# The front of layer 0: where U's loads, U's products and adj's first loads stand in a planned kernel

## The chip, the cores and the metric

The kernel runs on one core of one Trainium2 chip. The metric is the device time of one execution in microseconds (us), the median of several runs. The program has five engines that run side by side, each in the order of its own instruction queue: TensorE (PE, with its weight loads shown as PEld), VectorE (DVE), ScalarE (ACT), GpSimd (POOL), and SyncE (SP), which issues nearly all of the DMA transfers.

## What is computed

Two graph layers on 3327 nodes with 256 features, all in float32. In the program the nodes are padded to 26 row tiles of 128. Layer 0 is the layer that the change touches, and within it step n = 0 and what comes before it:

```python
h = maximum(layernorm(x), 0)                    # X, the input of layer 0
R = (adj + I) / rowsum(adj + I)
Xf = Xa = X;  Z = 0
for n in range(2):
    q = Xa @ W1.T @ W2.T;  k = Xa @ W3.T
    A = top_p(softmax(q @ k.T), 0.9)            # rows renormalised
    Xf = R @ Xf
    Xa = A @ Xa
    Z = Z + Xf @ U1[n].T + Xa @ U2[n].T
x = x + layernorm(X + Z)
...                                             # layer 1: masked attention over neighbours
```

## The kernel before, in words

**Order of the work.** The kernel is a list of pieces. Each piece is put into a plan with `put(engine, length, rank, fn, needs, take, give, lag)`: an assumed length, a rank (lower goes first), the pieces that it needs, the buffers that it takes and gives back, and a lag after its end until others may use its result. `Plan.order` (L507 on) then steps through assumed time: whenever an engine is free, it takes, of the pieces that are ready and whose buffers are free, the one with the lowest rank. The result is one fixed order per engine; on the chip each engine runs that order strictly, and waits on semaphores for what it really needs. `either` puts a piece that the plan gives to ACT or to DVE, whichever comes free for it first. So an assumed length, rank or lag changes no work, but changes the order in the queues.

**The front.** SP loads the 26 row tiles of x into `rhs` (`load_x`, L1962, rank -200 + t), with the two halves of U among them (in `weights`, L713 to L720; the trace shows the issue under L584): U1[0] and U1[1] side by side in `u1`, 128 x 2 x 512. ACT's queue loads W1, W2 and W3; PE and ACT make `wqk` of them (L724 to L745). For each row tile t there is then a chain: DVE measures mean and variance (L1213, L1214), POOL turns them into scale and bias in groups of 1 to 4 tiles (L1218 to L1221), ACT normalises and applies relu (L1239), PE transposes the tile into a `pl` bank (L1244), DVE copies it to `c[:, t]` (L1247), PE projects it to keys and queries in a `px` bank (L1252), ACT copies them to one of three `kq` buffers (L1258), POOL spreads the keys into `kt` (L1261), and SP stores or doubles the queries (L1269). A `kq` buffer comes back when POOL and SP are through with it. These pieces have rank -100 + t. Every fourth tile also goes through a small transpose and product in the two accumulator banks `acca` and `accf` (L789, L798, L808, L810).

**U's products.** Since R @ (X @ U) is (R @ X) @ U, the kernel multiplies the transposed tile `c[:, t]` by both halves of U first (`project_u`, L1304: four matmuls of 512 columns per tile, planned at 1.73 us). The left 256 columns of the result go to `main[:, t]`, the source of R's first product, and the right 256 over `c[:, t]`. The pieces of PE have rank -1.9 + 0.001 t: they fill PE's free time behind the chain of every tile and behind the logits of the first row (rank -2.5). The result stands in a `px` bank for t up to 7 and in `acca` or `accf` after that; ACT copies the left half (L1307), DVE the right half (L1308), both with rank -2.3.

**What follows.** `search` puts the logits of one row tile (L909) on PE, their exponentials and counts on ACT, DVE and POOL; `attention` multiplies the sparsified row by X (L1133) with `acca`; `full` multiplies a row tile of adj by `main` (L1158, 26 x 4 column groups of adj loaded by L1152 into six `at` buffers) with `accf`. `full` for n = 0 may load adj after all of the right-half copies of `project_u` (the argument `after`). SP loads U2 into the place of `u1` once the last of U's products is through (L747 to L752). 

**Idle work.** `idle` (L1966 to L1969) is a transpose of the identity into `accf` that nobody reads; 34 of these are put with rank 90, the last place in any choice, one after the other. They hold `accf` from the first to the last.

Of the kernel before, what the change touches and what calls it, by code (L numbers as in the profile page):

```python
# [19 lines left out]
P = 128  # L20
N = 3327
NT = 26
NP = NT * P
D = 256
# [563 lines left out]
def fast(  # L588
# [17 lines left out]
    nc = tc.nc  # L606
# [40 lines left out]
    with ExitStack() as l0:  # L647
# [53 lines left out]
        def weights():  # L701
            held = {}
            w1 = etpool.tile([P, 3 * D], F32, name="et")[:, : 4 * P].rearrange("p (a b) -> p a b", a=4)
            w1 = w1[:, 0, :].rearrange("p (c o) -> p c o", c=2)
            w2 = small.tile([P, PIECES, 8], F32, name="cands").rearrange("p c r -> p (c r)")[:DA, :DA]
            w1r = small.tile([P, PIECES * 8], F32, name="rest", bufs=1)[:DA].rearrange("p (k o) -> p k o", k=1)
            w1r = [w1r[:, 0, :], small.tile([P, P], F32, name="kq", bufs=BUFS["kq"])[:DA]]
            nc.scalar.dma_start(w1, w1t.rearrange("(c p) o -> p c o", p=P))
            nc.scalar.dma_start(w2, w2t)
            for r in range(2):  # L710
                nc.scalar.dma_start(wqk[:, :, r, r * DA : r * DA + DA], w3t.rearrange("(c p) o -> p c o", p=P))
            for n in range(STEPS):
                cols = slice((1 - n) * D, (2 - n) * D)  # L713
                uloads.append(
                    plan.put(
                        "SP", 0.4, -196.5 + n, nc.sync.dma_start, u1[:, :, cols],
                        u1t[n].rearrange("(c p) o -> p c o", p=P), lag=8.0,
                    )
                )

            S.activation(adds[:, 2:], powers[:, :1], AF.Exp)

            def turn():
                held["ps"] = ps_x.tile([DA, 2, P], F32, name="px")  # L724
                for k in range(2):
                    T.transpose(held["ps"][:, k, :], w1[:, k, :], ident)

            def copy():
                for k in range(2):
                    S.copy(w1r[k], held["ps"][:, k, :])  # L730

            def product():
                held["ps"] = ps_x.tile([P, 2, DA], F32, name="px")
                for k in range(2):
                    T.matmul(held["ps"][:, k, :], w1r[k], w2, start=True, stop=True)

            def place():
                for r in range(2):
                    S.copy(wqk[:, :, r, (1 - r) * DA : (2 - r) * DA], held["ps"])

            a = plan.put("PE", 0.25, -200.0, turn, take=["px"], needs=[plan.put("", 0.0, -201.0, lambda: None, lag=8.0)])
            a = plan.put("ACT", 0.5, -200.0, copy, needs=[a], take=["kq"], give=["px"])
            a = plan.put("PE", 0.25, -200.0, product, needs=[a], take=["px"], give=["kq"])
            return plan.put("ACT", 0.5, -200.0, place, needs=[a], give=["px"])
# [550 lines left out]
        def project_u(t, rank):  # L1295
            held = {}


            bank = ("acca", "accf")[t % 2] if t > 7 else "px"

            def product():
                ps = held["ps"] = (ps_x if bank == "px" else ps_a).tile([P, 2 * D], F32, name=bank)
                for k in range(2):
                    T.matmul(ps, c[:, t, k * P : (k + 1) * P], u1[:, k, :], start=(k == 0), stop=(k == 1))  # L1304

            a = plan.put("PE", 1.73, rank, product, needs=[turned_h[t], uloads], take=[bank])
            b = plan.put("ACT", 0.37, -2.3, lambda: S.copy(main[:, t, :D], held["ps"][:, :D]), needs=[a])  # L1307
            e = plan.put("DVE", 0.43, -2.3, lambda: V.tensor_copy(c[:, t, :], held["ps"][:, D:]), needs=[a])  # L1308
            plan.put("", 0.0, -2.6, lambda: None, needs=[b, e], give=[bank], lag=0.0)
            return b, e  # L1310

        def finish1(row, done, rank):
# [657 lines left out]

        spare = []
        a = plan.put("", 0.0, -202.0, lambda: None, lag=1.9)
        for k in range(34):
            a = plan.put("PE", 0.21, 90.0, idle, needs=[a], take=["accf"] * (k == 0), give=["accf"] * (k == 33), lag=0.0)

        uloads = []
        weighed = weights()
        loads = [plan.put("SP", 0.58, -200.0 + t, load_x, t) for t in range(NT)]
        measured = {}
        for lo, hi in zip(GROUPED, GROUPED[1:]):  # L1980
            measured.update(deviations(lo, hi))
# [8 lines left out]
        for n in range(STEPS):  # L1990
            base = 30.0 * n
            scaled = plan.put(
                "DVE", 0.2, base - 50.0,
                lambda gk=gks[n]: V.tensor_scalar(gk[:, : DA + 1], gk[:, : DA + 1], 1.0 / (-(-NT // 4) * P), None, ALU.mult), needs=[sums],
            )
            rows = [Row(n, i) for i in range(NT)]
            found = []
            held_by = []
            for g in range(GROUPS):
                lo, hi = 4 * g, min(4 * g + 4, NT)  # L2000
                r = base + lo - 6.0
                if n == 0 and g < 2:
                    q = saved[lo:hi]
                else:
                    q = plan.put(
                        "SP", 1.2, r, fetch_queries, n, g, needs=[saved[lo:hi], all_saved if n == 0 else None], take=["qg"], lag=3.0
                    )
                known, read = stats(n, lo, hi, base - 50.0 if g == 0 else r, [keys, q, fresh], scaled)
                found += [search(rows[t], base + t, [keys, q], known, fresh) for t in range(lo, hi)]
                plan.put("", 0.0, -90.0, lambda: None, needs=[read, [r.pieces["logits"] for r in rows[lo:hi]]], give=["qg"],  # L2010
                    lag=0.0,
                )
            if n == 0:
                drawn[0] = rows[-1].pieces["logits"]
            fulls = [
                full(n, t, (2.0 + 1.3 * t if n == 0 else base + 2.0 + 1.05 * t), [p[0] for p in sources], [p[1] for p in sources] if n == 0 else loaded[0])
                for t in range(NT)
            ]
            done = [attention(r, base + r.i, *found[r.i], right) for r in rows]
            failed.append(plan.put("DVE", 2.95, base + NT if n == 0 else 63.0, failures, n, needs=[[a for a, _ in found]]))  # L2020
            if n == 0:
                ends = [finish1(r, done[r.i], base + r.i + 0.2) for r in rows]
                stored = [y for _, _, _, y in ends]

                keys, after = [k for k, _, _, _ in ends], [drawn[0]]
                saved = [q for _, q, _, _ in ends]
                for r in range(2):
                    p = plan.put(
                        "SP", 1.3, base + NT, fetch_keys, r, needs=[after, saved[: LAST + 1]], lag=5.0
                    )  # L2030
                    keys.append(p)
                    after = [plan.put("", 0.0, -90.0, lambda: None, needs=[p], lag=0.0)]
                sums = [g for _, _, g, _ in ends]

                right, after = [], [done, stored]
                for lo in range(0, NT, 4):
                    hi = min(lo + 4, NT)
                    right.append(plan.put("SP", 0.1, base + NT, fetch_rhs, lo, hi, needs=after, lag=7.0))
                    after = [plan.put("", 0.0, -90.0, lambda: None, needs=right[-1:], lag=0.0)]
                fresh = failed + [r.pieces["guess"] for r in rows]  # L2040
                used, sources = sources, [(p,) for p in fulls]

                def layer1():
                    late["g"], late["b"], late["wa"], late["a"] = layer1_loads()

                    late["less"] = lambda: GP.tensor_scalar(late["b"], late["b"], -1.0, None, ALU.add)

                a = plan.put("SP", 1.8, base + NT + 1.0, layer1, needs=[used, stored], take=["et"], lag=8.0)
                less = plan.put("POOL", 0.6, base + 5.0, lambda: late["less"](), needs=[a])
                layer1_ready = plan.put(  # L2050
                    "DVE", 3.7, base + 5.0, lambda: layer1_scores(late["wa"], late["a"]), needs=[a], give=["et"],
                )
                layer1_ready = [layer1_ready, less]
            else:
                ends = [finish2(r, done[r.i], fulls[r.i], base + r.i + 0.2) for r in rows]
# [71 lines left out]
```

## Time and profile before

| what | value |
|---|---|
| median of 3 runs | 2057.34 us (2057.19 to 2058.23) |
| the profiled execution | 2056.36 us |
| its span, first to last instruction | 2054.5 us |
| PE busy | 2019.0 us, 98% of the span |
| DVE / ACT / POOL busy | 82% / 63% / 50% |
| granted TensorE clock, mean of the span | 0.998 |

The profile is one execution. A row gives the engine, the line of the kernel, the operation, output <- input, and how many; where it ends in square brackets, the engine stood idle so long before it, and the releaser that ended it follows. In the rows of a stretch, the busy time of each engine is followed by its instruction count, and then by PEclk, the granted TensorE clock (1.00 is full speed), the share of the DMA engines and what they moved. A PE instruction that is one of a run overlaps with the next, so the durations of single matmuls must not be added; the busy time of a stretch is a union and may be.

### The profile page before, as it was taken

To read this page: it belongs to the slowest core of one execution; us is meant where nothing else is said; L and a number is where in the kernel's file an instruction comes from. 1 tells how busy PE (TensorE), PEld (TensorE's weight loads), DVE (VectorE), ACT (ScalarE), POOL (GpSimd) and SP (SyncE) were. 2 spreads that over 40 slices of the span, in tenths; PEclk is the share of its full clock that TensorE was granted. 3 is DMA by queue.
4 is the path that set the end of the run, shared out by engine and by line. 5 is a ranking of instruction groups with operands and counts; after the bars stand their busy time and mean duration, and the time that the engine had idled before them with its cause. 6 is when DMAs were issued, how large, how long until landed. Compare 5 with 4: busy or idle time off the path is not lost. (4 is left out here: it accounts for less than half of the span.)

```text
span 2054.5 us, 34072 instructions
## 1 busy us (share of the span) xinstructions
PE 2019.0 (98%) x10545; PEld 1397.3 (68%) x10545; DVE 1691.5 (82%) x3753; ACT 1301.6 (63%) x2647; POOL 1029.3 (50%) x2222
## 2 busy tenths in 40 slices
PE   8999999999999999999999999999999999999997
PEld 6477877878777887788787787788877333333332
DVE  5488898888888854888887888978897999999894
ACT  4686667667576507884777787877643456474642
POOL 4366746565666504887766778877782000000001
PEclk9999999999999999999999999999999999999999
DMA  3177767767766776787676767766794354444440
GB/s 97 47 203 195 200 199 207 192 191 191 209 187 195 216 198 208 208 226 192 182 199 196 191 185 216 206 187 184 214 265 132 111 158 126 150 125 117 129 117 25
DMA packets 628991, 358.20 MB, mean 174 GB/s; under 512 B 366810, under 2 KB 581760, under 8 KB 628800
## 3 DMA queue, kind: packets, MB, share of 16 engines
q1 hardware_dynamic: 627904, 355.72, 61.6%
q8 instruction: 86, 1.41, 0.3%
q14 instruction: 105, 0.86, 0.1%
q10 hardware_dynamic: 896, 0.21, 0.0%
HBM read 252.69 MB, written 102.88 MB: 173 GB/s over the span
## 5 line engine op out<-in xcount | busy, mean ns | idle before, releaser
L964 ACT ACTIVATE junk<-e,sc 128x3327 fp8e5<-128x3327 f32 x147 | 451.0, 3068 | 62.7 <-POOL sc L1001 61.2
L1133 PE MATMUL acca<-rhs,e 128*128 128x256 f32 x2132 | 471.9, 380 | 3.6 <-DMA e<-blocks 3.5
L1133 PEld LDWEIGHTS acca<-rhs,e 128*128 128x128 f32 x2132 | 416.5, 196 | 50.2 <-issue 6.9
L1158 PE MATMUL accf<-main,at 128*128 128x257 f32 x1352 | 316.4, 383 | 7.4 <-ACT f L1169 2.6
L1158 PE MATMUL accf<-c,at 128*128 128x256 f32 x1352 | 308.4, 382 | 4.5 <-DVE main L1175 3.7
L1158 PEld LDWEIGHTS accf<-main,at 128*128 128x128 f32 x1352 | 249.9, 190 | 66.4 <-issue 18.9
L1158 PEld LDWEIGHTS accf<-c,at 128*128 128x128 f32 x1352 | 252.6, 190 | 54.0 <-issue 9.4
L1027 DVE MAX8 cands<-y 128x8 f32<-128x205 f32 (+1 forms) x832 | 242.8, 361 | 3.6
L1022 DVE SCALAR_TENSOR_TENSOR y<-e,sc 128x1639 f32<-128x1639 f32 x84 | 168.6, 2008 | 71.8 <-POOL sc L1012 70.8
L1738 ACT ACTIVATE junk<-at 128x448 bf16<-128x448 f32 (+1 forms) x204 | 112.2, 550 | 178.1 <-DVE e L1749 109.3
L1928 POOL TENSOR_TENSOR qq<-qq 128x256 f32<-128x256 f32 x4 | 2.9, 729 | 429.9 <-ACT qq L1924 429.9
L1765 PE MATMUL pl<-e,main 128*64 128x416 f32 x1024 | 192.2, 517 | 0.0
L909 PE MATMUL pl<-kt,qg 64*128 64x512 f32 (+1 forms) x832 | 174.2, 536 | 1.2 <-ACT e L926 1.0
L1078 DVE SCALAR_TENSOR_TENSOR e<-e,thr 128x1024 f32<-128x1024 f32 (+1 forms) x126 | 172.8, 1373 | 1.3 <-DVE rest L1072 0.4
L1117 DVE STREAM_TRANSPOSE e<-e 128x1024 f32<-128x1024 f32 (+1 forms) x123 | 164.5, 1338 | 7.2 <-POOL sc L1004 0.5
L926 ACT ACTIVATE e<-pl 128x1024 f32<-128x1024 f32 x123 | 134.7, 1105 | 53.2 <-PE pl L909 50.0
L1765 PEld LDWEIGHTS pl<-e,main 128*64 128x64 f32 x1024 | 69.0, 137 | 109.5 <-issue 91.7
L1749 DVE SCALAR_TENSOR_TENSOR e<-qq,low,junk 128x832 f32<-128x832 f32 x128 | 129.5, 1076 | 4.4 <-ACT junk L1738 2.8
L1749 DVE SCALAR_TENSOR_TENSOR e<-c,low,junk 128x832 f32<-128x832 f32 x128 | 129.1, 1071 | 4.2 <-issue 3.2
L909 PEld LDWEIGHTS pl<-kt,qg 64*128 64x128 f32 x832 | 71.3, 186 | 87.5 <-issue 72.4
L1133 PE MATMUL acca<-rhs,qq 128*128 128x256 f32 x520 | 115.0, 380 | 0.3 <-DVE thr L1069 0.3
L1737 ACT ACTIVATE at<-at 128x448 f32<-128x448 f32 (+1 forms) x204 | 110.3, 540 | 0.0
(554 smaller groups left out, 3375.4 us busy)
## 6 DMA issues: line engine op xcount, KB each, us to landing
at<-in_adjt_dram SPq DMA_DIRECT2D x414, 256.0 KB
blocks<-e SPq DMA_DIRECT2D x82, 512.0 KB
e<-blocks SPq DMA_DIRECT2D x328, 128.0 KB
blocks<-e SPq DMA_DIRECT2D x41, 640.0 KB
e<-blocks SPq DMA_DIRECT2D x164, 160.0 KB
at<-in_adjt_dram SPq DMA_DIRECT2D x102, 192.0 KB
blocks<-qq SPq DMA_DIRECT2D x20, 512.0 KB
qq<-blocks SPq DMA_DIRECT2D x80, 128.0 KB
```

The source lines that it names most:

```text
L909: T.matmul(pl[:, lo : lo + m], qg[self.n, self.i // 4][half, self.i % 4, :], kt[half, 512 * k : 512 * k + m], start=True, stop=True,)
L926: S.activation(to, pl.rearrange("p (g t q) -> p g t q", g=4, t=2), AF.Exp, accum_out=sums[k])
L964: S.activation(junk[:, :N], self.e[:, :N], fn, bias=t, scale=-1.0, accum_out=dst, saturate=False)
L1022: V.scalar_tensor_tensor(self.y[:, : hi - lo], self.e[:, lo:hi], self.up, self.e[:, lo:hi], ALU.is_lt, ALU.mult, accum_out=(self.h0, self. ...
L1027: V.max(self.cands[:, a * PIECES // 2 + k, :], self.y[:, at[k] - lo : at[k + 1] - lo])
L1078: V.scalar_tensor_tensor(piece, piece, self.thr[:, at : at + 1], piece, ALU.is_gt, ALU.mult)
L1117: V.transpose(part, part)
L1133: T.matmul(self.acc, lhs, rhs[self.n][:, j, :], start=(j == 0), stop=(j == NT - 1))
L1158: T.matmul(self.acc[:, : self.w], self.at[j // JC][:, j % JC, :], self.src[:, j, : self.w], start=(j == 0), stop=(j == NT - 1),)
L1738: S.activation(to, src, AF.Sign)
L1749: V.scalar_tensor_tensor(held["e"][:, k, :], extra["both"][b % 2][:, k, :], low[:, j, k : k + 1], held["mask"], ALU.max, ALU.mult,)
L1765: T.matmul(q["acc"][a][k * FH : (k + 1) * FH, c, :C], main[:, j, h * FH : (h + 1) * FH], held["e"][:, h, c * C : (c + 1) * C], start=(j == 0),
```

## The change

It reorders the front, in five places. U's two loads go behind the second tile of x, ahead of the third, and the plan is told shorter lags for them, for x and for W1. U's results all go to `acca` and `accf` in turn, none to `px`. Their two copies get ranks t - 97, next to the chains of tiles t to t + 3, and each may go to ACT or to DVE; the empty piece that gives the bank back goes to rank -300. The idle transposes are 15 in place of 34. And adj's loads for n = 0 need the stored queries (`saved`) in place of U's right-half copies.

```diff
@@ weights
                     plan.put(
-                        "SP", 0.4, -196.5 + n, nc.sync.dma_start, u1[:, :, cols],
-                        u1t[n].rearrange("(c p) o -> p c o", p=P), lag=8.0,
+                        "SP", 0.4, -198.5 + 0.1 * n, nc.sync.dma_start, u1[:, :, cols],
+                        u1t[n].rearrange("(c p) o -> p c o", p=P), lag=4.5,
                     )
...
-            a = plan.put("PE", 0.25, -200.0, turn, take=["px"], needs=[plan.put("", 0.0, -201.0, lambda: None, lag=8.0)])
+            a = plan.put("PE", 0.25, -200.0, turn, take=["px"], needs=[plan.put("", 0.0, -201.0, lambda: None, lag=5.0)])
@@ project_u
-            bank = ("acca", "accf")[t % 2] if t > 7 else "px"
+            bank = ("acca", "accf")[t % 2]
...
             a = plan.put("PE", 1.73, rank, product, needs=[turned_h[t], uloads], take=[bank])
-            b = plan.put("ACT", 0.37, -2.3, lambda: S.copy(main[:, t, :D], held["ps"][:, :D]), needs=[a])
-            e = plan.put("DVE", 0.43, -2.3, lambda: V.tensor_copy(c[:, t, :], held["ps"][:, D:]), needs=[a])
-            plan.put("", 0.0, -2.6, lambda: None, needs=[b, e], give=[bank], lag=0.0)
+            b, e = (
+                plan.either(
+                    ("ACT", 0.37, lambda to=to, k=k: S.copy(to[:, t, :D], held["ps"][:, k * D : (k + 1) * D])),
+                    ("DVE", 0.43, lambda to=to, k=k: V.tensor_copy(to[:, t, :D], held["ps"][:, k * D : (k + 1) * D])),
+                    t - 97.0, needs=[a],
+                )
+                for k, to in enumerate((main, c))
+            )
+            plan.put("", 0.0, -300.0, lambda: None, needs=[b, e], give=[bank], lag=0.0)
             return b, e
@@ fast
-        for k in range(34):
-            a = plan.put("PE", 0.21, 90.0, idle, needs=[a], take=["accf"] * (k == 0), give=["accf"] * (k == 33), lag=0.0)
+        for k in range(15):
+            a = plan.put("PE", 0.21, 90.0, idle, needs=[a], take=["accf"] * (k == 0), give=["accf"] * (k == 14), lag=0.0)
...
-        loads = [plan.put("SP", 0.58, -200.0 + t, load_x, t) for t in range(NT)]
+        loads = [plan.put("SP", 0.48, -200.0 + t, load_x, t, lag=2.2 if t < 2 else 3.5) for t in range(NT)]
...
-                full(n, t, (2.0 + 1.3 * t if n == 0 else base + 2.0 + 1.05 * t), [p[0] for p in sources], [p[1] for p in sources] if n == 0 else loaded[0])
+                full(n, t, (2.0 + 1.3 * t if n == 0 else base + 2.0 + 1.05 * t), [p[0] for p in sources], saved if n == 0 else loaded[0])
```

## The prediction

> **What bounds the kernel now.** I read the page's busy shares and slices first: PE 98%, near full clock everywhere. So the stage rows come next; then the front by stretches, the waits of PE in it, and its PE queue in order of time.
>
> Stretches of the whole span, PE's busy time being the second figure:
>
> ```profile
> 0.00:5.91 5.91, 3.69 (x19) 3.45 (x19) 1.99 (x7) 2.09 (x3) 3.58 (x26) 1.00 0.62 164
> 5.91:97.77 91.86, 83.99 (x359) 47.57 (x359) 45.41 (x167) 53.38 (x140) 36.76 (x105) 0.98 0.22 63
> ```
> ```profile
> 100.00:750.00 650.00, 645.32 (x2962) 510.01 (x2961) 552.55 (x1384) 424.73 (x800) 389.47 (x844) 1.00 0.72 201
> 750.00:820.00 70.00, 69.87 (x327) 55.23 (x328) 22.15 (x86) 37.66 (x74) 23.59 (x55) 1.00 0.60 182
> 820.00:1520.00 700.00, 690.76 (x3200) 564.55 (x3198) 588.43 (x1501) 512.38 (x970) 536.42 (x1143) 1.00 0.73 200
> ```
>
> The reader is to see that PE stands 4.7 us in 650, 0.1 in 70 and 9.2 in 700, but 7.9 us (91.86 less 83.99) in the 92 us of the front. The end is PE's work plus PE's standing time. The row of 750 to 820 says that this also holds where the two steps meet: DVE has only 22 us of work there and PE is full, since products of `full` left over from step 0 still run. A search that begins some us sooner or later is covered by these; a PE microsecond saved in the front is saved at the end.
>
> Not all busy time of the front is work. PE's queue there, and the stretch around it (granted clock third from the right):
>
> ```profile
> 6.19 0.82 PE L1969 MATMUL accf<-ident 128*128 128x128 f32 x6
> ...
> 18.34 3.58 PE L1304 MATMUL acca<-late,c 128*128 128x512 f32 x4
> ...
> 23.08 1.88 PE L1304 MATMUL accf<-late,c 128*128 128x512 f32 x4
> ```
> ```profile
> 4.65:8.06 3.41, 2.52 (x20) 2.04 (x19) 1.73 (x7) 1.20 (x2) 2.71 (x9) 1.00 0.99 293
> ...
> 14.89:18.30 3.41, 1.98 (x15) 1.34 (x13) 2.89 (x13) 1.58 (x3) 2.95 (x9) 1.00 0.65 203
> 18.30:21.72 3.42, 3.42 (x6) 1.38 (x5) 2.79 (x11) 1.90 (x5) 2.15 (x8) 0.50 0.07 17
> ```
>
> The same four matmuls take 3.58 us at half clock and 1.88 at full; the half clock follows a stretch in which PE was busy 1.98 of 3.41 us, 58%. And the waits of PE from 5.9 to 98:
>
> ```profile
> PE accf L1158 <- DVE cands L1027: 2.4, 1, 2.4
> PE pl L1244 <- ACT rhs L1239: 2.2, 4, 0.9
> PE pl L1244 <- DVE bst L1213: 1.1, 1, 1.1
> PE pl L909 <- ACT e L926: 1.0, 1, 1.0
> ```
>
> The first is put down to a DVE instruction that has nothing to do with `accf`; what came last is adj's first tile: SP issues it at 92.08 and `full` starts at 97.77.
>
> **What can be saved.** From PE's first useful matmul (5.91) to the first one of `full` (97.77): standing 7.9; 15 idle transposes at some 0.14 us each (six in 0.82), 2.1; half clock, half of 3.4 us, 1.7. Together 11.7 us. What lies ahead of 5.91 (x's first tile, its statistics on DVE, POOL, ACT) the change leaves alone.
>
> **The change part by part.**
>
> *U's loads and W1's lag.* Before, the first product of U runs at 18.34, though `c` holds a tile from 8.35 on (the copy of 7.96): up to t = 7 the products need a `px` bank, which the chains of rank -100 take first. After: the two loads are issued at about 1.7 and 2.1 (x's issues are 0.45 us apart from 0.72); x2, issued about there now, is used 3.4 us later (4.99), so I put their landing near 5.5. The shorter assumed loads and lags of x move nothing by themselves but the order, and are costed with it. Tile 0 is normalised at 5.26 to 5.86, transposed by 6.35; its copy stands behind tile 2's statistics on DVE. I put the first product at 7.4. The loads are moved past x2 and x3 on SP (one also past x4): two issues of 0.38 us and 512 KB at the 290 GB/s of these stretches, 1.8 us for x2 and x3, 0.9 for x4, nothing from x5 on. The statistics of x2 so come at about 6.5 instead of 4.99, those of x4 at 7.33 as before. The cover is the first products, 1.7 us each; without them PE would stand those 1.8 us. W1's turn (7.84) and `wqk` (12.0) come some 3 us sooner; their transfers have long landed, since no row shows PE waiting for them.
>
> *Products as filler from 7.4 on.* Work per tile on PE: 0.39 (L1244: 10.2 over 26), 0.56 (L1252: 14.6 over 26) and 1.73, so 2.7 us. DVE needs 1.0 us per tile (0.41, 0.18, 0.41), ACT 0.86, the loads 0.45. Tiles come more than twice as fast as PE can use them, so standing in 8 to 22 should nearly vanish, and with it the half clock at 18.3 and the idle transposes. The 26 products are the same work as before, only sooner.
>
> *Banks.* The products lose `px`, which 8 of 26 used, most of them at 68 to 82. With two banks, one comes back after left and right copy one behind the other (0.37 and 0.42 us, DVE's mostly waiting for ACT's), about 1.0 us after the product; a cycle of 2.8 us on two banks, one product per 1.4, is less than the 1.73 that PE needs. So the cost is nothing while the copies are prompt. Where ACT is in a count of 3.07 us (L964), or DVE in one of 1.95 (L1022), a copy may come up to 3 us late, and PE stands for what exceeds 0.7. Bounds: 0 (81.9 to 91 runs on `acca` and `accf` alone, and stands nowhere) and 3 counts at 2.3, some 7. The nearest row is the first; I take 0.6.
>
> *Copies with rank t - 97.* The same 52 copies. New is who is queued behind them: a copy whose product isn't ended holds up the relu, the `kq` copy and the statistics of later tiles on its engine. Before, ACT waited 12.7 us for products in 0 to 60 (13 copies; 1.0 each). The price lies between nothing (PE has turned tiles in stock) and the rival below; I take 0.7 of PE time.
>
> *Idle transposes, 34 to 15.* They end at 1.78 + 15 x 0.19 = 4.6 instead of 5.47, and none fills 6 to 10. The Trainium skill (TensorE: Matmul & The Clock Gate, "Part 4: PE-mode transpose") says that transposes do not count as PE activity for the clock; by that, taking 19 away costs nothing. The trace disagrees: from 1.78 to 11.9 PE runs hardly anything but transposes and is granted 1.00 all through. So they count, and from 4.6 to 8.0 PE would have only some 1.3 us of tile 0, tile 1 and W1 and 0.6 of the first product, under 60%, like 14.89 to 18.30, which was followed by half clock. The same page's table in "Why this matters for your kernels" asks only for no gaps over about 3 us; by that no drop, by the row one drop of 3.4 us, 1.7 lost. I take the row: 1.7, bounds 0 and two stretches, 3.4.
>
> *adj's first loads.* Six issues move from 92 to behind the last query store, about 55, ahead of U2's two on SP. DMA share there is 0.00 to 0.16, so 1.5 MB are hidden. U2's loads still wait for the last product; behind them stand only loads whose `at` buffers are free no sooner. The 2.4 us go; the 1.0 before the logits too, since `full` can run there. Next late is the single bank of `full`, 0.5 us at a change of row tile: one more of these, 0.5.
>
> **Sum.** Left over: idle before the first product 0.2 to 0.8, taken 0.5; banks 0.6; copies 0.7; clock 1.7; bank of `full` 0.5: 4.0. Gain 11.7 - 4.0 = 7.7 us. The profiled execution (2054.5 of span and 1.86 around it) goes from 2056.4 to 2048.7; the median is 1.0 above the profiled one, so 2049.6. Everything behind is planned anew from other times; its 14 us of standing (4.7 + 0.1 + 9.2) may move by 4 either way.
>
> **Rivals.** *It does less than it says:* tiles reach `c` late, for DVE is in order and its statistics wait for x (5.3 us of that in the trace), so the holes of 8 to 18 stay; only adj's part (3.4) and half the transposes (1.0) count: 2057.3 - 4.4, 2053. For: DVE is 2.9 of 3.4 us busy in 8 to 18; against: its copies already come at 8, 9.8, 10.7, 12.1. *Nothing is left to lose in the front:* no clock drop and the steps pack better by 3 us: 2045. *Slower: the copies block the chain.* If each pair makes ACT stand 1 us in the stretch of the chains, 26 us come on top of ACT's 22 us of relu and `kq` copies in 5 to 40, 48 in 35: PE starves 13 us, against 7.7 gained, 2063. It decides from the point where waiting on ACT exceeds the 13 us that it has free, half of the pairs. For: strict queues, and the wait is there now; against: `either` spreads it over two engines, and product work covers it.
>
> **Numbers.** Forecast 2049.6, 50%; less than it says, 2053, 22%; everything, 2045, 14%; slower or given back later, 2058 to 2063, 14%. Range 2044.5 to 2057.5. A difference under 0.2% (4.1 us) can't be told from none: faster 0.74, same 0.14, slower 0.12.
>
> **What would show it.** Right: L1304 first at 7 to 8; PE busy over 95% from 8 to 22; no wait of `accf` L1158 near the end of the front; that first matmul at 89 to 91; a half clock, if any, before 12. Wrong: PE waiting in front of L1244 for ACT with copies of L1307's kind queued there; PE waiting for bank copies behind L964; or a front shorter by 8 us and standing in 100 to 1520 grown by as much.

## The result, and the profile after

| | before | after |
|---|---|---|
| median on one chip, 9 runs each | 2057.34 us (2055.35 to 2060.71) | 2050.47 us (2049.43 to 2054.74) |
| the profiled execution | 2056.36 us | 2050.93 us |
| its span | 2054.5 us | 2049.1 us |
| PE busy | 2019.0 us | 2017.5 us |
| granted TensorE clock, mean of the span | 0.998 | 0.996 |

The ratio is 0.9966, with a 95% interval of 0.9958 to 0.9975: the changed kernel is faster by 6.9 us in the medians and by 5.4 in the two profiled executions. The forecast was 2049.6. In the kernel after, lines behind L1304 stand some lines further down: the idle transposes are L1975, U's copies L1309 (ACT) and L1310 (DVE), layer 1's products L1771 (L1765 before).

PE's queue in the front of the kernel after, in order of time:

```profile
1.78 3.25 PE L1975 MATMUL accf<-ident 128*128 128x128 f32 x15 [1.78 <-POOL ident masks.py:199]
4.87 0.38 PE L726 MATMUL px<-ident,et 128*64 128x128 f32 x2
...
7.80 3.53 PE L1304 MATMUL acca<-late,c 128*128 128x512 f32 x4 [0.90 <-DVE c L1247]
...
14.13 1.95 PE L1304 MATMUL accf<-late,c 128*128 128x512 f32 x4
```

The first product of U runs at 7.80 (18.34 before), and it is the one that falls into the half clock: its four matmuls take 3.53 us, where those of the next take 1.95. The waits of PE from 0 to 100 us, with the total, the number and the longest:

```profile
PE accf L1975 <- POOL ident masks.py:199: 1.8, 1, 1.8
PE acca L1304 <- DVE c L1247: 0.9, 1, 0.9
PE pl L1244 <- ACT rhs L1239: 0.6, 1, 0.6
PE accf L1158 <- ACT f L1169: 0.5, 1, 0.5
PE acca L789 <- ACT kq L1258: 0.4, 1, 0.4
```

The 2.4 us of `accf` at the front's end are gone; the 0.5 is a change of `full`'s row tile at 99.17, behind the front. The same stretches as before the change (the front ends at the first product of `full`, now at 83.55):

```profile
5.88:83.55 77.67, 76.26 (x326) 44.35 (x326) 37.86 (x149) 47.22 (x123) 31.33 (x92) 0.98 0.25 73
...
100.00:750.00 650.00, 647.79 (x2980) 514.42 (x2979) 548.29 (x1373) 420.14 (x796) 403.04 (x841) 1.00 0.73 202
750.00:820.00 70.00, 68.42 (x320) 51.42 (x319) 32.45 (x104) 46.05 (x87) 32.15 (x73) 1.00 0.60 179
820.00:1520.00 700.00, 691.58 (x3204) 565.94 (x3201) 585.56 (x1492) 505.03 (x949) 520.14 (x1133) 1.00 0.73 201
1520.00:1580.00 60.00, 55.47 (x284) 41.94 (x284) 43.15 (x104) 18.88 (x52) 19.53 (x30) 0.94 0.50 149
```

PE stands 1.4 us in the front (77.67 less 76.26), against 7.9. The rows behind move by little, except the last: where layer 1 begins, PE stands 4.5 us in 60 and runs at a mean clock of 0.94. The same row of the kernel before:

```profile
1520.00:1580.00 60.00, 59.22 (x292) 47.40 (x292) 45.60 (x101) 20.66 (x55) 26.83 (x37) 1.00 0.58 169
```

So the time has this account, in us of PE, for the two profiled executions. The stretches end at the first product of `full` in step 0, at 750, at the first product of `full` in step 1, at 1500, where layer 1's steady products begin, and at the last product, each at its own time in each kernel. The columns give what PE stands in them, and what the half clock that the profile shows costs while PE is busy:

| stretch | standing before | standing after | half clock before | half clock after |
|---|---|---|---|---|
| start to first `full` | 10.1 | 3.8 | 1.7 | 1.7 |
| to 750 | 4.7 | 2.7 | 0 | 0 |
| to step 1's first `full` | 1.1 | 2.7 | 0 | 0 |
| to 1500 | 7.8 | 7.3 | 0 | 0 |
| to layer 1's steady part | 1.3 | 4.5 | 0 | 3.0 |
| rest, up to the last product | 1.8 | 1.8 | 0 | 0 |

In the front 6.3 us of standing are gone, and with 34 idle transposes become 15, some 2.9 us of their time (in PE's queue 3.69 + 0.82 + 0.38 + 0.60 + 0.27 + 0.44 before, 3.25 after): 9.2. At the start of layer 1, 3.2 of standing and 3.0 of half clock come on top: 6.2. The stretches between give 0.9. That makes 3.9 of the 5.4; the other 1.5 lie in busy time that I can't place, as the ends of matmuls are modelled.

**The new stall.** PE's queue there:

```profile
1522.48 1.99 PE L1158 MATMUL accf<-c,at 128*128 128x256 f32 x8 [0.56 <-ACT main L1172]
1527.91 11.80 PE L1133 MATMUL acca<-rhs,e 128*128 128x256 f32 x40 [3.43 <-DMA e<-blocks]
```

and SP's queue of DMA issues in the same stretch:

```profile
1506.04 2.07 SPq L1721 DMA_DIRECT2D kt<-in_adjt_dram  x4
1508.16 0.94 SPq L1688 DMA_DIRECT2D qq<-highs  x2
...
1518.19 0.60 SPq L1152 DMA_DIRECT2D at<-in_adjt_dram  x1
1519.52 7.84 SPq L1126 DMA_DIRECT2D e<-blocks  x8
1527.46 0.43 SPq L1152 DMA_DIRECT2D at<-in_adjt_dram  x1
```

Layer 1's first loads (L1721, L1688) go out some 9 us earlier than before (1515.31). The DMA engines are full (392 GB/s at a share of 1.05 from 1515 to 1520), and the eight issues of `e<-blocks` take SP 7.84 us. PE runs its queue strictly in order: what stands next in it at 1524.5 is `attention`, which waits for `e`, and the next product of `full` stands behind it, at 1543.26. The kernel before has DMA engines as full from 1525 to 1530 (393 GB/s at 1.06) and yet waits only 0.45 us for `e`; its queue has 16 matmuls of layer 1 (3.0 us from 1531.73) ahead of `attention` there. After the stall PE runs at half clock from 1527.9 to 1533.8, which costs half of these 5.9 us. Not every execution need have that: the mean granted clock of the nine lies between 0.996 and 0.998, and 0.002 of 2049 us are 4 us.

### The profile page after: what moved, and what is told of

Its sections match the earlier page's. It is cut to its first block, busy times and chain, and to the rows that moved or that the text cites. A ratio compares the mean times of both kernels' runs of the same rounds, so it can differ in the third digit from the quotient of the medians.

```text
span 2049.1 us, 33972 instructions
## 1 busy us (share of the span) xinstructions
PE 2017.5 (98%) x10526; PEld 1398.1 (68%) x10526; DVE 1688.8 (82%) x3763; ACT 1298.0 (63%) x2637; POOL 1025.8 (50%) x2222
## 5 line engine op out<-in xcount | busy, mean ns | idle before, releaser
L1771 PE MATMUL pl<-e,main 128*64 128x416 f32 x1024 | 191.9, 517 | 0.0
L1771 PEld LDWEIGHTS pl<-e,main 128*64 128x64 f32 x1024 | 69.5, 137 | 109.4 <-issue 91.8
L964 ACT ACTIVATE junk<-qq,sc 128x3327 fp8e5<-128x3327 f32 x35 | 107.4, 3068 | 19.5 <-POOL sc L1001 19.2
```

The lines of the kernel that those rows point to most:

```text
L964: S.activation(junk[:, :N], self.e[:, :N], fn, bias=t, scale=-1.0, accum_out=dst, saturate=False)
L1771: T.matmul(q["acc"][a][k * FH : (k + 1) * FH, c, :C], main[:, j, h * FH : (h + 1) * FH], held["e"][:, h, c * C : (c + 1) * C], start=(j == 0),
```

## The experiments

The theory: the products of U fill PE's holes behind the chains, which needs early loads, two banks that come back at once, and so prompt copies; what the front gains is partly lost behind, where the plan is another. The rivals: adj's early loads alone are what counts; the banks or the copies cost something that the front hides; or the difference is mostly that of one plan against another. Beside each experiment the kernel before ran on the same chip; a ratio is against it. Standing and clock are from one profiled execution of each.

**adj's loads late again (e1).**

```diff
-    ..., saved if n == 0 else loaded[0])
+    ..., [p[1] for p in sources] if n == 0 else loaded[0])
```

> The changed kernel, but adj's first loads wait again for U's right-half copies. Theory (what counts is the time for which PE stands or idles in the front, and each part of the change takes its own share away): the loads are issued near 80 instead of 55, PE stands for some 2 us before the first product of full, the median is about 2 us above the changed kernel, 2052.5. Rival (the gain comes from the plan behind the front, which merely fell better): the front's standing hardly moves the end, and the median may lie anywhere within 4 us of the changed kernel.

Measured 2046.65 us (2046.04 to 2049.24), ratio 0.9958, interval 0.9945 to 0.9970: not slower than the whole change. In the trace its front does stand more, 6.0 us against 3.8, and the first product of `full` is at 89.4; but the stall at 1524 is not there (1.9 us of standing in that stretch, no half clock). So the theory's 2.1 us are there in the front, and are paid back behind.

**adj's loads early, and nothing else (e2).** The kernel before with the edit of e1 the other way round.

> The kernel before, with adj's first loads behind the stored queries and nothing else of the change. Theory: the 2.4 us of standing before the first product of full go and at most 1.0 more before the logits, so 2054 to 2055 instead of 2057.3. Rival (plan luck): no tie to 2.4 us, anything from 2053 to 2061.

Measured 2048.28 us (2046.46 to 2050.72), ratio 0.9968, interval 0.9956 to 0.9980: as much as the whole change. The front stands 6.0 us in place of 10.1, and the stretch to 750 1.9 in place of 4.7. Of the first, 4.1 us, the two waits that the edit was to end are 3.4 (2.4 and 1.0); the other 0.7 lie ahead of 80 us, where PE's order is that of before (at the start, for one, the idle transposes run slower, 19 in 4.32 us against 3.69, and so fill more). The second is a plan that happens to pack better. That adj's loads alone are what counts is not so either, since e1, without them, is as fast. Its front holds something that I had not expected. PE's order up to here is that of before, yet:

```profile
18.41 1.88 PE L1304 MATMUL acca<-late,c 128*128 128x512 f32 x4
```

The stretch ahead of it is as empty as before (PE busy 1.98 of 3.41 us in both), and no half clock follows; the part on the clock comes back to it.

**U's loads late (e3).**

```diff
-    "SP", 0.4, -198.5 + 0.1 * n, ... lag=4.5,
+    "SP", 0.4, -196.5 + n, ... lag=8.0,
```

> The changed kernel with U's loads at their old places among x (behind the fourth and fifth tile) and their old assumed lag. Theory: the first product of U comes near 12 to 13 instead of 7.8, and what PE stands or runs at half clock between 6 and 16 grows by 2 to 3 us, so 2052.5 to 2053.5. Rival (U's loads don't matter, since the tiles are what is late): the first product stays where it is relative to the chains and the time stays within 1 us, 2050 to 2051.5.

Measured 2049.56 us (2047.95 to 2050.62), ratio 0.9967, interval 0.9954 to 0.9980. The first product of U moves to 13.41, and still the front stands 3.7 us, as without this edit (3.8). Behind it, up to 750, this run stands 6.7 us in place of 2.7 and has a second half clock, from 102.1 to 105.5; at the start of layer 1 it lacks the stall. That the early place of the loads brings anything is not shown.

**The copies last, as before (e4).** Fixed engines and rank -2.3:

```diff
-    b, e = ( plan.either(... t - 97.0, needs=[a]) ... )
-    plan.put("", 0.0, -300.0, lambda: None, needs=[b, e], give=[bank], lag=0.0)
+    b = plan.put("ACT", 0.37, -2.3, ...)
+    e = plan.put("DVE", 0.43, -2.3, ...)
+    plan.put("", 0.0, -2.6, lambda: None, needs=[b, e], give=[bank], lag=0.0)
```

> The changed kernel with the old copies: left half on ACT, right half on DVE, both with rank -2.3, behind all chains. Theory (products are filler, and the copies decide when a bank is free again): the two banks stay taken while the chains run, PE finds no product to fill with between 16 and 25, and stands there 3 to 5 us more; 2053.5 to 2055.5. Rival (copies in their turn cost the chain as much as they bring the products): within 1 us of the changed kernel.

Measured 2057.82 us (2053.55 to 2062.43), ratio 1.0011, interval 1.0004 to 1.0017: the gain is gone, and the front stands 10.5 us. First of this kernel, then of the one after, the stretch from 20 to 36:

```profile
20.00:36.00 16.00, 11.97 (x54) 7.60 (x54) 11.60 (x40) 8.58 (x20) 8.73 (x25) 0.79 0.07 14
```
```profile
20.00:36.00 16.00, 15.97 (x85) 10.62 (x84) 12.13 (x44) 11.12 (x32) 10.58 (x31) 1.00 0.11 23
```

and the matmuls of U's products (L1304 alone) that each runs from 5 to 40, first in e4 and then in the kernel after:

```profile
5.00:40.00 35.00, 12.70 (x20) 4.26 (x20) 0.85 0.37 107
```
```profile
5.00:40.00 35.00, 18.66 (x36) 6.48 (x36) 0.95 0.39 112
```

With the copies behind everything else, the banks don't come back. Only 20 of the 104 matmuls fill the holes, about as many as before the change (18), against 36; PE stands 4 of 16 us, and another half clock comes, from 29.1 to 36.0. Of the single edits tried, this is the only one whose removal takes the whole gain.

**The first products back in `px` (e5).**

```diff
-    bank = ("acca", "accf")[t % 2]
+    bank = ("acca", "accf")[t % 2] if t > 7 else "px"
```

> The changed kernel with the first eight tiles' products of U in px again, as before the change; copies, loads and idle work as changed. Theory (with copies in their turn two banks are enough, so the px banks bring nothing): standing in the front within 1 us of the changed kernel's 3.8 us up to the first product of full. The end may differ by up to 4 us by the plan behind the front alone, as the run with adj loaded late has shown. Rival (the products in px were what kept the projections waiting): standing in the front grows by 3 us or more.

Measured 2044.05 us (2042.23 to 2044.66), ratio 0.9941, interval 0.9927 to 0.9954: faster than both kernels. Its front stands about as long (4.1 us) and shows no half clock; the stretches to step 1's first `full` stand 3.0 us in place of 5.4, and the start of layer 1 3.0 us, without half clock. Of the 8.5 us between the two profiled executions, 4.7 are half clock (1.7 in the front, 3.0 at the stall) and 2.3 are standing.

**PE's gaps filled (e6), and one idle transpose in place of 15 (e7).** e6 puts idle transposes where PE stood, e7 takes them away:

```diff
@@ e6: weights, in W1's turn() and in product()
+                for _ in range(4):      # turn
+                    T.transpose(spare[0], ident, ident)
+                for _ in range(5):      # product
+                    T.transpose(spare[0], ident, ident)
@@ e7: fast
-        for k in range(15):
+        for k in range(1):
```

> The changed kernel with nine more idle transposes in PE's two holes ahead of the first product of U, put into existing pieces so that the plan is the same everywhere. Theory (transposes count as activity for the clock, and the half clock of 8.2 to 11.5 follows from the thin stretch before it): granted clock 1.00 from 8 to 12, the products of 7.8 take 1.9 instead of 3.5 us, the front 1.7 us shorter, the median 1 to 1.7 us below the changed kernel's, which is 6.9 us below the kernel before; so 8 to 8.6 below it. Rival (transposes don't count): the half clock stays, and the time.

> The changed kernel with one idle transpose instead of 15, the plan of all other pieces being the same. Theory (transposes count): the granted clock falls before 8 us, near 5, and stays at a half until 11.5; since the products of 7.8 ran at half clock anyway, the end is the same within 1 us, 5.9 to 6.9 below the kernel before. Rival (transposes don't count, and it is the first real matmuls that decide): rows of the clock as in the changed kernel, full until 8.2.

Measured 2047.73 us (2046.91 to 2049.98; ratio 0.9962, interval 0.9948 to 0.9975) and 2047.91 us (2044.88 to 2050.57; 0.9960, 0.9946 to 0.9973). Their first product of U, in e6 and in e7:

```profile
7.87 1.88 PE L1308 MATMUL acca<-late,c 128*128 128x512 f32 x4
```
```profile
8.49 3.78 PE L1304 MATMUL acca<-late,c 128*128 128x512 f32 x4 [0.82 <-DVE c L1247]
```

With the gaps filled the clock stays full there, and these four matmuls take 1.9 us less than in e7; the two medians are alike all the same. That the filling did it is not shown: e5, with the gaps open, has the same four at full clock too (1.98 us at 7.97). Both runs have PE's order of the kernel after to the end, and both have its stall: 3.01 us at 1526.33 in e6 and 3.14 at 1527.27 in e7, each ended by `e<-blocks`.

**Layer 1's heads held back (e8).** If the stall comes from layer 1's loads in the DMA engines, it should go when layer 1's first heads wait for the last `e` of the row before the last:

```diff
-    got, after = [], [spread[: b + 1], opened[b % 2], used_heads[b % 2]]
+    got, after = [], [spread[: b + 1], opened[b % 2], used_heads[b % 2], rows[NT - 2].pieces["got"] if b == 0 else None]
```

> The changed kernel with layer 1's first broadcast of the heads (0.85 MB written to SBUF per transfer, two of them) held back until step 1's last blocked row tile has been fetched again from memory. Theory (those transfers stood ahead of a row's blocks on the DMA queues, PE stood 3.4 us for them at 1524.5 and then ran at half clock): no standing over 1.5 us at this place, full clock there, and the end 4 to 5 us sooner, 11 to 12 below the kernel before. Rival (PE stood there because the plan had nothing left to fill with): a wait of 3 us or more stays or moves to the next row, and the time stays within 2 us of the changed kernel.

Measured 2053.98 us (2051.18 to 2055.69), ratio 0.9989, interval 0.9982 to 0.9995: worse than the kernel after. The wait for `e<-blocks` does fall from 3.4 to 0.38 us, but further on in PE's queue stands

```profile
1522.33 7.15 PE L1133 MATMUL acca<-rhs,e 128*128 128x256 f32 x32 [0.38 <-DMA e<-blocks]
1542.55 0.69 PE L1440 MATMUL px<-ident,xa 128*128 128x128 f32 x2 [7.33 <-ACT xa L1435]
```

Layer 1's first products, eight of them (1.74 us) at 1518.5 in the kernel after, come only at 1568.3. PE stands from 1535.2 to 1542.55 because its next instruction needs the end of a row of layer 0 (`xa`). My reading of the stall as DMA traffic alone is thereby wrong: the wait for `e` went, and a longer one came. How much of the 7.3 us layer 1's products would have filled is not shown; before this place only 1.74 us of them ran in the kernel after.

**Another plan behind the same front (e9 after, e10 before).** One rank of step 1, a hundredth apart. PE's order is unchanged up to 1116 us in e9 and up to 1353 in e10.

```diff
-    base + 2.0 + 1.05 * t
+    base + 2.0 + 1.06 * t
```

> The changed kernel with one assumed rank of step 1 altered: the products of full go by 1.06 per row tile instead of 1.05. PE's order is the same up to the second half of step 1. Theory (the 3.4 us of standing at 1524.5 belong to how this one plan fell: adj's loads stood in SP's queue behind a row's fetches; every other order seen lacks it): no wait over 2 us between steps and layer 1, and the median 3 to 5 us below the changed kernel's, 10 to 12 below the kernel before. Rival (whoever saves time in the front meets layer 1's first loads there): the wait stays over 2.5 us, 6 to 8 below the kernel before.

> The kernel before with the same altered rank of step 1, and nothing of the change. It measures how much the plan behind the front moves by itself. Theory: such an edit moves the median by up to 3 us either way without anything in the front, so a single comparison of two plans is uncertain by about that; 2053 to 2059, with standing from 895 to 1580 within 3 us of the kernel before's 9.1. Rival (the plan behind the front is steady, and the other runs' gains all came from the front): within 0.7 us of the kernel before.

Measured 2052.46 us (2050.64 to 2054.81; ratio 0.9975, interval 0.9965 to 0.9985) and 2063.32 us (2059.07 to 2070.19; 1.0031, 1.0019 to 1.0042), with the kernel before at 2057.63 on that chip. The rank, which touches nothing of the front, makes the kernel before 5.7 us slower. In e10 the loss is where layer 1 starts: 5.8 us of standing there in place of 1.3. Both of my numbers missed. In e9 the single stall is gone, but from 1500 to 1580 PE stands 5.5 us in smaller waits (1.9 for `e<-blocks`, 2.2 for DVE in front of layer 1's products, 0.7 for adj, 0.6 for ACT), and the stretch from step 1's first `full` to 1500 stands 9.7 in place of 7.3. With this rank in both kernels the change brings 10.9 us, with the old rank 6.9.

**`px` with the gaps filled (e11), and with adj's loads late (e12).** The edits of e5 and e6 together, and of e5 and e1.

> The changed kernel with U's first eight products in px and with nine idle transposes in PE's two early holes; the plan is that of the run with px alone. Theory (the early half clock comes and goes with the phase of the clock's window, and costs 1.7 us when it comes; filled holes keep it away): a median within 1 us of the run with px, 12 below the kernel before, and full-speed durations of the first product of U, 1.9 us for the four. Rival: the fillers delay the first products by their own 1.3 us, and the median is 1 us higher.

> The run with U's first eight products in px, but adj's first loads again behind U's right-half copies. Theory (adj's part is worth what PE stands at the end of the front, here about 2 us since logits fill some of it, and no more): standing up to the first product of full 2 us above the run with px (6 against 4.1), the median 1 to 3 us above it. Rival (adj's part is covered by logits that take its place): the same time within 1 us.

Measured 2044.16 us (2042.12 to 2048.29; ratio 0.9937, interval 0.9925 to 0.9949) and 2045.90 us (2043.06 to 2048.97; 0.9941, 0.9928 to 0.9954). With `px`, adj late stands 1.6 us more in the front (5.7 against 4.1), and the medians differ by 1.9, the ratios not at all. Together with e5 there are now three pairs whose edits differ in the banks alone. In ratio, `px` is ahead by 0.0025 (e5 and after), 0.0025 (e11 and e6) and 0.0017 (e12 and e1, whose intervals overlap), 3.5 to 5.1 us of 2057. But PE's order is one and the same in e5 and e11, and one and the same in the kernel after, e6 and e7, so the three pairs compare only two pairs of plans, and one rank alone moved 5.7 us. The fronts of the pairs differ by at most 0.4 us of standing, and the kernel after and e6 have the stall at layer 1, with 3.0 and 2.9 us of half clock, where e5 and e11 have none. So it isn't shown that the banks themselves cost anything: the plan that comes with them may.

## Why the prediction was right, and where it was not

*What bounds the kernel.* Right for the front: the sum of what can be saved there, 11.7 us, holds; 7.9 of standing became 1.4, the transposes behind 5.9 went, and the half clock stayed. But that a microsecond saved in the front is saved at the end was wrong: 6.2 us came back at the start of layer 1, and e1, whose front stands 2.1 us more, ends no later. The row of 750 to 820, on which I had rested it, stands 1.6 us in the kernel after (70.00 less 68.42), against 0.1.

*Products as filler from 7.4 on.* Right: 7.80; PE is busy 13.59 of the 14 us from 8 to 22, 97%, against 11.16 before. e4 shows that the copies carry it.

*U's loads.* That their cost to x2 and x3 is covered fits the 3.8 us of the front. That they must be early is not borne out: e3, with a first product at 13.41, stands as little there.

*Banks and copies, 0.6 and 0.7.* In the front both are smaller: no wait for a bank, and 0.4 for a `kq` copy. ACT does stand more for products in the first 60 us (17.7 us in 13 waits, against 12.7 in 8), but PE is covered. Two counts in the prediction's working were off: the 12.7 us belong to 10 copies of L1307 and not to 13, and the relu and `kq` copies keep ACT busy for 18.7 us (14.54 and 4.13) from 5 to 40, not for 22. Ahead of the first product stand 0.9 us (forecast 0.5), and 0.5 at `full`'s change of row tile, as forecast. The left-over so is 0.9 + 0.4 + 1.7 + 0.5 = 3.5, against 4.0. This term looked at the front alone; what the banks do to the plan behind is the open point of the pairs with `px`.

*Idle transposes and clock.* The size was right, 1.7, and the place too, 8.1 to 11.5. The ground is not shown, and the place is partly luck. First, the granted clock of 1.00 from 1.78 on, which I set against the Trainium skill's sentence on transposes, is no evidence: in e7 and e9 the row of 8 to 9 reads 1.00 too, while four matmuls take 3.78 us, twice their 1.88. The durations are. These are the idle transposes of the kernel before from 1.7 to 4.5 us and from 4.8 to 7.1, with the shortest, the median and the longest in ns:

```profile
L1969 PE MATMUL accf<-ident x13: 414/421/476, 1.8 to 4.4; 128*128 128x128 f32 x13
```
```profile
L1969 PE MATMUL accf<-ident x13: 272/273/414, 4.4 to 6.7; 128*128 128x128 f32 x13
```

PE had run nothing but transposes when it came to full speed, so they do count here, and the measurement decides. They did not suffice every time: by such durations, twelve of the thirteen profiled executions with 15 or more transposes are at full speed by 7.3 us, but e9, with the front order of the kernel after, only at about 14, and e7, with one transpose, at about 13.

Second, the stretch that decides. In each trace the granted clock changes only at times that lie whole multiples of 3.41 us apart (in the kernel after at 8.09, 11.50, 1527.02 and 1533.85), so each execution is divided into steps of that length, and the division lies elsewhere in each. In the kernel before, the step ahead of the drop is 14.91 to 18.33, the stretch of 58%; in the kernel after it is 4.68 to 8.09, with PE busy 1.89 us, 55%. In e2 the only change that the rows show is at 2037.96. Carried back in steps of 3.4133 us (in the kernel after, 445 of them make the 1518.93 us from 8.09 to 1527.02), the steps of its front are:

```profile
10.45:13.86 3.41, 2.26 (x18) 1.78 (x18) 3.17 (x12) 2.40 (x8) 2.07 (x8) 1.00 0.90 268
13.86:17.27 3.41, 2.34 (x20) 2.00 (x18) 2.75 (x11) 1.85 (x6) 2.89 (x10) 1.00 0.79 252
```

PE is busy 66% and 69% in these. The same order of PE is divided elsewhere here, and no step of the front at full clock is as empty as 58%, so e2 does not contradict the row that I took. But 60% of a step is no limit either. In e10, whose clock drops at 11.75, the steps give

```profile
8.34:11.75 3.41, 2.38 (x16) 1.46 (x14) 2.46 (x9) 1.57 (x5) 1.70 (x6) 1.00 0.90 284
11.75:15.16 3.41, 2.92 (x14) 2.92 (x15) 2.05 (x9) 2.55 (x8) 2.06 (x7) 0.50 0.94 265
...
93.67:97.08 3.41, 1.54 (x8) 0.39 (x4) 3.38 (x9) 2.10 (x7) 2.80 (x6) 1.00 0.99 288
97.08:100.50 3.42, 2.87 (x13) 2.53 (x14) 3.04 (x17) 3.32 (x10) 1.93 (x8) 1.00 0.52 198
```

a half clock behind 70%, and none behind 45%. The step of 70% holds mostly transposes, that of 45% none; by what PE's activity is measured is not shown. The bound of the Trainium skill (TensorE: Matmul & The Clock Gate, "Why this matters for your kernels": no gaps over about 3 us) fits the stall of 3.43 at 1527 and its half clock, but not the drop at 8.1, whose longest gap ahead is 0.9.

*adj's first loads.* The wait went, as forecast. The first product of `full` came at 83.55 and not at 89 to 91, because 16 fewer matmuls of the logits, 3.2 us, run ahead of it; counted for that it is 86.8, 11 us earlier than 97.77 and still 2 to 4 before the place that I named.

*What lies behind.* "May move by 4 either way" was the right kind of term, but too small: the start of layer 1 took 6.2, and e10 moved 5.7 with the front left alone. The case that I had named as the sign of being wrong, a front shorter by 8 us and as much given back, came true by more than half, though the place is not 100 to 1520 but just behind it. That the median hit within 0.9 us is thus in good part luck: a front better than forecast by about 1.5 us (9.2 against 7.7), a loss of 6.2 behind that my sum did not contain, 2.4 on the other side (the 0.9 and the unplaced 1.5 above), and a difference of medians that happens to be 1.5 larger than that of the two profiled executions.

*The rivals.* "The copies block the chain" did not happen: PE waits 0.6 us for `rhs` (L1239) in the front, not 13. "Does less than it says" fell: the holes closed. "Everything" (2045) is the time that e5 shows, with the banks undone.

What stays open: by what measure of PE's activity the clock drops; whether the 3.5 to 5.1 us of the `px` pairs are the banks or the plans; and how the 6.9 us divide among the other edits, since the plan behind moves as much as each of them. e1, e2 and e3 cannot be told from the whole change. That the copies must be prompt is shown, by e4, in the front's own standing; of the other parts none is shown to be needed for the median.

## What to carry to other kernels

Early work fills holes only if its results leave their buffers at once: give the copies that free a bank the turn of the work that they stand beside, not the lowest rank. In a kernel whose order comes from a planner, read an edit by the standing time of its own stretch, and try it under a second plan before believing a difference of less than some 6 us in 2050. Where a stage ends and PE is short of work, taking one wait away may only open another: with a later stage's loads held back to spare the DMA engines, a wait of 3.4 us became one of 7.3.

## What the runs showed of the hardware that was not expected

- The granted clock changed only at whole steps of 3.41 us, laid differently in each execution. The same order of PE so met a half clock at 18.33 us in the kernel before (3.58 us for four 512-column float32 matmuls), at 11.75 in e10, and none in e2 (1.88).
- The granted clock in the profile can read 1.00 while matmuls run at half speed at the start of an execution: 3.78 us for those four at 8.49 in e7 and at 8.71 in e9. Until the first change of clock shows, the durations are the better witness.
- Transposes alone brought PE to full speed (421 ns each, then 273, in the kernel before).
- SP's issues of `e<-blocks` from 1519.5 to 1529.4 took from 0.33 to 2.03 us each. The DMA engines were full (a share of 1.02 from 1519.5 to 1527.5), but that this holds the issues is not shown: at a share of 1.05 four of them took 2.49 us in the kernel before.
